# A two-layer gated transformer block: router norm statistics on ScalarE, the last keys and V evicted there, and a V projection two slots later

## The chip, the cores and the metric

The kernel runs on one core of one Trainium2 chip. The core has a matrix engine (TensorE, PE in the profile; its weight loads are the row PEld), a vector engine (VectorE, DVE), an engine for pointwise functions (ScalarE, ACT), a general one (GpSimd, POOL) and a queue that only issues transfers (SyncE, SP). Each works through its own queue of instructions in order and waits for others by semaphores. Matmul results go to PSUM, of which this kernel uses eight banks of 128 x 512 floats. The metric is the device time of one execution, in microseconds (us).

## What is computed

Four batch elements of 512 tokens, 256 features, 16 heads of 16, pass through two layers. Everything is fp32.

```python
x = x + tanh(g_xattn[0]) * L0_xattn(layernorm(x), ctx, ctx, ...)   # softmax attention with a decay bias
x = x + tanh(g_ffn[0])   * L0_ffn(layernorm(x), ...)               # ternary weights, ReLU, 256 -> 1024 -> 256
x = x + tanh(g_xattn[1]) * L1_xattn(layernorm(x), ctx, ctx, ...)   # q, k and v pass through ReLU
x = x + tanh(g_ffn[1])   * L1_ffn(layernorm(x), ...)               # four experts, top 1, gelu, then a norm

# L1_xattn
qp, kp, vp = relu(q @ Wq.T), relu(k @ Wk.T), relu(v @ Wv.T)
A = softmax(NORM * einsum('bqhd,bkhd->bhqk', qh, kh))
# L1_ffn: the normalized x chooses the expert
logits = x @ W_router
expert_idx = argmax(logits, axis=-1)
# the layernorm in front of each part
m, v = mean(x), var(x)
(x - m) / sqrt(v + 1e-5)
```

The part that the change touches is in the second layer: the norm in front of the router (its mean and variance), the projections of keys and values, and where one of the value projections stands.

## The kernel before

**The loop.** Heads are taken in 32 groups, four for each batch element b of each layer, and a group has four units, so 128 units in all. The main loop runs over u from -4 to 127. In each pass `scores` issues two "quads" of score matmuls for TensorE. A quad holds two matmuls `pm` (scores of a unit six ahead, of which only the row maximum is wanted) and two matmuls `psc` (scores of this unit, which become attention weights). Each score matmul is only 32 rows deep[...]. After a quad come its drains: VectorE reduces each pm to a maximum (L508, `tensor_reduce`), and ScalarE turns each psc into exponentials (L523). After the scores `slot(u)` issues the other work of the pass: in every fourth pass `weighted` (the product of weights and V, called po, L551, copied to oT by ScalarE), two passes later `shifted` (pmT, maxima turned and subtracted from q) and `divided` (pn, the quotient o, added to x), and then jobs from chains.

**Chains.** A chain is a list of jobs (function, cost, gap) with the pass in which it may start and the pass by which it must end. `slot` takes jobs whose time has come, the one due first first, as long as their costs fit into 3.1 us; overdue jobs are taken regardless. The order on every engine is thus the order in which the Python code issues instructions: nothing reorders them later. For the second layer, batch b has its first unit at u0 = 64 + 16 b. The chain of its norm (statistics in two halves, rows, transposes) and of the projection of its first keys and queries may start at u0 - 14; the chain `values`, with two halves of V, may start at u0 - 8 and ends by u0 + 2. The router chain `route(b)` starts at four passes (b = 2: two passes) after the last unit of batch b: first half of the statistics, second half, rows, transposes, logits, ranks. The router of the last batch, b = 3, runs behind the loop.

**Statistics.** `layernorm` returns three jobs. The first two read two row tiles each with `bn_stats` and `bn_aggr` on VectorE (L325, L326). The second ends with `deviations`, some eight small operations of GpSimd on 128 x 4 values that make `rstd` and `off` (minus mean times rstd). The third, on ScalarE (L356), writes the normalized rows: four instructions of 128 x 256.

**PSUM banks.** `bank_psum` takes the next of eight banks in turn, so every product waits until the one eight banks earlier has been read out. Two jobs put two results into one bank and have two engines read it: `values` (L433 on ScalarE, L435 on VectorE, one row tile each) and the keys (`key_half`, L463 on ScalarE and L465 on VectorE, one mask each).

**The passes concerned.** V of batch 2 in u=95. The norm of batch 3, and behind it the router of batch 1, in u=98 to 104, together with the first keys and queries of batch 3 (u=102 and 103). V of batch 3 in u=105 and 106, its second keys in u=109. The router of batch 2 from u=114 on, beside the first matmuls of the experts (pg, L996, copied by ScalarE to ha, L1001).

Of the kernel before, what the change touches and what calls it, by code (L numbers as in the profile page):

```python
# [48 lines left out]
def flamingo_kernel(ctx: ExitStack, tc: tile.TileContext, t: dict, out: bass.AP):  # L49
# [260 lines left out]
        ]  # L310


    def layernorm(src, dst, eps, name, eng=None, meanwhile=None):

        mv = sml.tile([P, NT, 2], F32, tag="mv", name=f"mv_{name}")
        var, rstd, fix, off = (
            sml.tile([P, NT], F32, tag=v, name=f"{v}_{name}") for v in ("var", "rstd", "fix", "off")
        )  # L320

        def half_stats(n0):
            for n in range(n0, n0 + NT // 2):
                st = sml.tile([P, 6], F32, tag="st", name=f"st_{name}{n}")
                nc.vector.bn_stats(st, src[:, n, :])  # L325
                nc.vector.bn_aggr(mv[:, n, :], st)  # L326

        def deviations():

            (nc.vector if meanwhile else nc.gpsimd).tensor_scalar(  # L330
                var, mv[:, :, 1], eps, None, ALU.add
            )
            nc.gpsimd.tensor_tensor(rstd, var, power, ALU.pow)
            if meanwhile:
                meanwhile()
            g = nc.vector if meanwhile else nc.gpsimd
            g.tensor_tensor(fix, rstd, rstd, ALU.mult)
            g.tensor_tensor(fix, fix, var, ALU.mult)
            g.tensor_scalar(fix, fix, -0.5, 1.5, ALU.mult, ALU.add)
            g.tensor_tensor(rstd, rstd, fix, ALU.mult)  # L340
            if eng is None:
                nc.gpsimd.tensor_scalar(off, mv[:, :, 0], -1.0, None, ALU.mult)
                nc.gpsimd.tensor_tensor(off, off, rstd, ALU.mult)

        def first():
            half_stats(0)

        def second():
            half_stats(NT // 2)
            deviations()  # L350

        def rows_(dst=dst):
            for n in range(NT):
                r = rstd[:, n : n + 1]
                if eng is None:
                    nc.scalar.activation(  # L356
                        dst[:, n, :], src[:, n, :], AF.Identity, bias=off[:, n : n + 1], scale=r
                    )
                else:
                    eng.tensor_scalar(  # L360
                        dst[:, n, :], src[:, n, :], mv[:, n, 0:1], r, ALU.subtract, ALU.mult
                    )

        return first, second, rows_
# [26 lines left out]
    def prepare(layer, b, eng=None, meanwhile=None):  # L391

        nm = f"a{layer}_{b}"
        st = {}

        def stats():
            st["xn"] = act.tile([P, NT, D], F32, tag="xn", name=f"xn_{nm}")
            first, st["more"], st["rows"] = layernorm(
                x[b], st["xn"], 1e-5, nm, eng, meanwhile
            )  # L400
            first()

        def more_stats():
            st["more"]()

        def norm():
            st["rows"]()

        def turn():
            xTs[layer, b] = act.tile([P, NC, S], F32, tag="xT", name=f"xT_{nm}", bufs=2)  # L410
            transposed(st["xn"], xTs[layer, b], nm, layer == 0 and b > 0)

        def values(n0):
            def run():
                wv = attn_w[layer]["wv"]
                vh = v_sb[b % 2][1]
                pv = bank_psum(f"pv{nm}{n0}")
                for n in range(2):
                    for c in range(NC):
                        nc.tensor.matmul(  # L420
                            pv[:, ts(n, D)], lhsT=cT[b][:, c, ts(n0 + n, P)], rhs=wv[:, c, :],
                            start=(c == 0), stop=(c == NC - 1),
                        )
                if layer == 0:
                    nc.scalar.copy(
                        vh[:, n0 : n0 + 2, :, 0:DK], pv.rearrange("p (n h d) -> p n h d", n=2, d=DK)
                    )
                    return
                for n in range(2):
                    to = vh[:, n0 + n, :, 0:DK]  # L430
                    of = pv[:, ts(n, D)].rearrange("p (h d) -> p h d", d=DK)
                    if n == 0:
                        nc.scalar.activation(to, of, AF.Relu)  # L433
                    else:
                        nc.vector.tensor_scalar(to, of, 0.0, None, ALU.max)  # L435

            return run

        return (
            [(stats, 0, 0), (more_stats, 0, 1), (norm, 0, 1), (turn, 0.9, 1)],  # L440
            [(values(0), 1.75, 0), (values(2), 1.75, 0)],
        )

    def project(layer, b, tt):

        nm = f"{layer}_{b}{tt}"

        def product(w, src, name):
            pp = bank_psum(f"{name}{nm}")
            for c in range(NC):  # L450
                nc.tensor.matmul(  # L451
                    pp, lhsT=attn_w[layer][w][:, c, ts(tt, P)], rhs=src[:, c, :],
                    start=(c == 0), stop=(c == NC - 1),
                )
            return pp

        def key_half(pk, e):
            k = act.tile([P, S], F32, tag="k", name=f"k{nm}{e}", bufs=5)
            h = half[:, e : e + 1]
            if layer == 0:  # L460
                nc.vector.scalar_tensor_tensor(k, pk, h, kext[tt, e], ALU.mult, ALU.add)
            elif e == 0:
                nc.scalar.activation(k, pk, AF.Relu, bias=kone[:, e : e + 1], scale=h)  # L463
            else:
                nc.vector.tensor_scalar(k, pk, h, kone[:, e : e + 1], ALU.mult, ALU.max)  # L465
            ks[layer, b, tt, e] = k

        def keys(between=None, halves=range(2)):
            pk = product("wk", cT[b], "pk")
            if between:  # L470
                between()
            for e in halves:
                key_half(pk, e)

        def queries():
            pq = product("wq", xTs[layer, b], "pq")
            for e in range(2):
                q = act.tile([P, S], F32, tag="q", name=f"q{nm}{e}", bufs=4)
                h = half[:, e : e + 1]
                if layer == 0 and (e == 0 or b < 2):  # L480
                    nc.scalar.activation(q, pq, AF.Identity, bias=bqk[:, 0, tt, e : e + 1], scale=h)  # L481
                elif layer == 0:
                    nc.vector.tensor_scalar(q, pq, h, bqk[:, 0, tt, e : e + 1], ALU.mult, ALU.add)
                elif e == 0:
                    nc.scalar.activation(q, pq, AF.Relu, scale=h)
                else:
                    nc.vector.tensor_scalar(q, pq, h, 0.0, ALU.mult, ALU.max)
                qs[layer, b, tt, e] = q

        return [(keys, 1.75, 1), (queries, 1.75, 0)]  # L490
# [214 lines left out]
    def route(b, eng=None):  # L705
# [3 lines left out]
        def stats():  # L709
            st["xn"] = act.tile([P, NT, D], F32, tag="xn", name=f"xn_f1_{b}")  # L710
            first, st["more"], st["rows"] = layernorm(
                x[b], st["xn"], 1e-5, f"f1_{b}", eng
            )
            first()

# [305 lines left out]
    def chain(steps, start, end, *after):  # L1021
        last = [end] * len(steps)
        for i in range(len(steps) - 2, -1, -1):
            last[i] = last[i + 1] - max(steps[i + 1][2], 1 if steps[i][1] and steps[i + 1][1] else 0)
        c = dict(steps=list(zip(steps, last)), ready=start, after=after, done=None)
        chains.append(c)
        return c
# [12 lines left out]
    for layer in range(2):  # L1040
        for b in range(B):
            u0 = first_unit(layer, b)
            lead, values = prepare(layer, b)
            if (layer, b) == (0, 1):
                *early, early_rows, turn_1 = (job for job, *_ in lead)
                (early_values, *_), later_values = values
                turned_1 = chain([later_values, (turn_1, 0.9, 1)], 1, 4)
                chain(project(layer, b, 0), 5, u0 - LEAD - 2, turned_1)
            elif u0:
                chain(  # L1050
                    [*lead, *project(layer, b, 0)], u0 - 14, u0 - LEAD - 2,
                    ffns[b] if layer else None,
                )
                chain(values, u0 - 8, u0 + 2)
            chain(project(layer, b, 1), max(u0 - 4, 0), u0)
    (totals1, *_), *quant1 = quantize(w1f, "w1")
    (totals2, *_), *quant2 = quantize(w2f, "w2")
# [291 lines left out]
```

## Time and profile before

| what | us |
|---|---|
| median of three runs | 862.4 (861.65 to 863.38) |
| the profiled execution | 861.21 |
| its span, from the first to the last instruction | 859.5 |
| reductions of pm, L508, 512 of 682 ns | 316.9 busy |
| exponentials of psc, L523, 512 of 602 ns | 267.1 busy |
| `bn_stats` of the router norms, L325, 32 of 406 ns | 13.0 busy |
| `bn_aggr` of the same, L326, 32 of 182 ns | 5.8 busy |
| second key halves, L465, 8 of 810 ns | 6.5 busy |
| second V halves, L435, 8 of 424 ns | 3.4 busy |

A line of groups gives source line, engine and operation, what is written from what, the shape and the count; behind the bar stand the busy time in us, the mean ns of one, and the idle time of the engine before it with what ended it. A line of the timeline gives start and duration in us, then the same names. A line of the busy times by stretch gives start and end, length, and for each engine busy time and number of instructions. A line of waits gives who waited for whom, the sum in us, how often, and the longest. Matmul ends are modelled, and a busy PE isn't a PE at its peak.

### The profile page before, as it was taken

How to read it: one execution, taken by the hardware profiler on the slowest of the kernel's cores; microseconds unless marked ns; L12 is line 12 of the kernel's file. 1: busy time of each engine (PE TensorE's matmuls, PEld its weight loads, DVE VectorE, ACT ScalarE, POOL GpSimd, SP SyncE). 2: the span in 40 equal slices, each digit the busy share in tenths (PEclk: the TensorE clock that was granted, in tenths of full speed). 3: DMA queues.
4: the chain of work that ended last, by engine and by line, in shares of the span. 5: the costliest groups of instructions: out<-in, count | busy, mean ns of one | idle time of the engine just before them, and what ended most of it. 6: DMA issues, size and time to landing. Idle time of an engine off the chain costs nothing. (4 is left out here: it accounts for less than half of the span.)

```text
span 859.5 us, 13597 instructions
## 1 busy us (share of the span) xinstructions
PE 821.1 (96%) x5241; PEld 462.1 (54%) x5241; DVE 561.7 (65%) x1218; ACT 422.5 (49%) x886; POOL 277.4 (32%) x446
## 2 busy tenths in 40 slices
PE   6999999999999999999999999999999996999994
PEld 3444454445464346445554445634545655888993
DVE  6878778766857784768646865577877645753443
ACT  2576475553555452655435563357556564223331
POOL 5536365424342422311100120012033216244542
PEclk9999999999999999999999999999999998899998
DMA  8100000000000000000000010001032328136540
GB/s 312 64 1 1 1 2 2 1 1 0 2 13 25 1 1 0 26 0 2 1 1 25 1 50 1 1 1 50 1 119 96 106 75 292 40 93 233 195 155 14
DMA packets 18096, 43.07 MB, mean 50 GB/s; under 512 B 2222, under 2 KB 12208, under 8 KB 15600
## 3 DMA queue, kind: packets, MB, share of 16 engines
q0 software_dynamic: 5488, 28.13, 9.6%
q1 hardware_dynamic: 12128, 13.54, 4.7%
q8 instruction: 41, 0.67, 0.3%
q10 hardware_dynamic: 416, 0.54, 0.2%
q14 instruction: 23, 0.19, 0.1%
HBM read 35.91 MB, written 6.68 MB: 50 GB/s over the span
## 5 line engine op out<-in xcount | busy, mean ns | idle before, releaser
L508 DVE TENSOR_REDUCE m<-pm 128x1 f32<-128x512 f32 x512 | 316.9, 682 | 107.6 <-PE psc L494 105.2
L523 ACT ACTIVATE p<-psc 128x512 f32<-128x512 f32 x512 | 267.1, 602 | 150.9 <-PE psc L494 148.3
L494 PE MATMUL psc<-q,k 32*128 32x512 f32 x1024 | 279.5, 622 | 0.2 <-DVE h L672 0.2
L494 PE MATMUL pm<-k,q 32*128 32x512 f32 x1024 | 262.1, 615 | 1.3 <-ACT q L481 0.9
L526 POOL TENSOR_TENSOR p<-p,dec 128x256 f32<-128x256 f32 x128 | 93.6, 735 | 177.2 <-ACT p L523 177.2
L494 PEld LDWEIGHTS pm<-k,q 32*128 32x128 f32 x1024 | 92.7, 184 | 83.5 <-issue 50.0
L494 PEld LDWEIGHTS psc<-q,k 32*128 32x128 f32 x1024 | 106.6, 183 | 52.2 <-issue 25.7
L551 PE MATMUL po<-p,v 128*32 128x512 f32 x1024 | 116.5, 595 | 1.9 <-DVE m L508 1.9
L551 PEld LDWEIGHTS po<-p,v 128*32 128x32 f32 x1024 | 31.7, 109 | 81.8 <-issue 60.8
L996 PE MATMUL pg<-xs,wg 128*128 128x128 f32 x608 | 72.4, 276 | 1.8 <-ACT xs L977 1.3
L996 PEld LDWEIGHTS pg<-xs,wg 128*128 128x128 f32 x608 | 70.5, 192 | 5.9 <-issue 1.7
L1178 PE MATMUL pyf<-wo,ha 128*128 128x256 f32 x304 | 70.3, 387 | 0.0
L1009 ACT ACTIVATE ha<-pg,wg 128x128 f32<-128x128 f32 x120 | 34.2, 368 | 69.6 <-PE pg L996 66.8
L619 POOL TENSOR_TENSOR x<-x,o 128x256 f32<-128x256 f32 x14 | 10.2, 729 | 174.4 <-DVE o L612 131.7
L1178 PEld LDWEIGHTS pyf<-wo,ha 128*128 128x128 f32 x304 | 57.9, 195 | 7.5
L664 PE MATMUL ph<-xTf,w1q 128*128 128x512 f32 x128 | 60.0, 605 | 0.0
L379 PE MATMUL py_f<-w2q,h 128*128 128x256 f32 x256 | 57.2, 381 | 0.0
L557 ACT COPY oT<-po 128x512 f32<-128x512 f32 x32 | 18.7, 584 | 77.6 <-PE po L551 77.6
L379 PEld LDWEIGHTS py_f<-w2q,h 128*128 128x128 f32 x256 | 48.0, 190 | 9.4 <-DVE m L508 3.0
L451 PE MATMUL pk<-cT,wk 128*128 128x512 f32 x68 | 35.3, 644 | 7.2 <-DMA cT<-in_ctxT_dram 7.2
L1182 DVE TENSOR_TENSOR y<-y,pyf 128x256 f32<-128x256 f32 x19 | 8.0, 421 | 47.4 <-PE pyf L1178 43.4
L664 PEld LDWEIGHTS ph<-xTf,w1q 128*128 128x128 f32 x128 | 22.6, 189 | 30.4 <-issue 18.2
(223 smaller groups left out, 810.1 us busy)
## 6 DMA issues: line engine op xcount, KB each, us to landing
x<-in_x_dram SPq DMA_DIRECT2D x4, 512.0 KB, 7.0
rows_d<-xn_f SPq DMA_DIRECT2D x4, 512.0 KB, 3.0
rows_d<-x SPq DMA_DIRECT2D x4, 512.0 KB, 3.1
cT<-in_ctxT_dram SPq DMA_DIRECT2D x3, 512.0 KB, 9.5
w1q<-in_w_dram SPq DMA_DIRECT2D x1, 1024.0 KB
w2q<-in_w_dram SPq DMA_DIRECT2D x1, 1024.0 KB, 11.3
wo<-in_wo_dram SPq DMA_DIRECT2D x2, 512.0 KB
rows<-in_rows_dram SPq DMA_DIRECT2D x1, 640.0 KB, 9.2
```

The costliest lines, as they stand in the source:

```text
L379: nc.tensor.matmul(py[:, n, :], lhsT=operand(c, n0 + n), rhs=w[:, c, :], start=(c == 0), stop=(c == chunks - 1),)
L451: nc.tensor.matmul(pp, lhsT=attn_w[layer][w][:, c, ts(tt, P)], rhs=src[:, c, :], start=(c == 0), stop=(c == NC - 1),)
L494: nc.tensor.matmul(out_, lhsT=lhs[r, ts(n, P)], rhs=rhs[r, :], start=True, stop=True)
L508: nc.vector.tensor_reduce(m[:, n, 2 * pair + i, r : r + 1], pm[i], AX.X, ALU.max)
L523: nc.scalar.activation(p[:, i, :], psc[i], AF.Exp, scale=SCALE)
L526: nc.gpsimd.tensor_tensor(d, d, dec.unsqueeze(1).to_broadcast([P, 2, P]), ALU.mult)
L551: nc.tensor.matmul(po[i * HP : (i + 1) * HP, :], lhsT=v_sb[b % 2][0][:, kt, c0 : c0 + HP], rhs=ps_exp[NT * s + kt, i // 2][:, i % 2, :], s ...
L557: nc.scalar.copy(pos[s], po)
L664: nc.tensor.matmul(ph, lhsT=w1q[:, c, ts(f, P)], rhs=st["xT"][:, c, :], start=(c == 0), stop=(c == NC - 1),)
L996: nc.tensor.matmul(ph[:, f, :], lhsT=w[:, c, ts(f2 * NF // 2 + f, P)], rhs=xs[j][:, c, :], start=(c == 0), stop=(c == NC - 1),)
L1009: nc.scalar.activation(ha[:, f, :], (ha if src is None else src)[:, f, :], AF.Gelu, bias=biases[j][:, fa : fa + 1],)
L1178: nc.tensor.matmul(py, lhsT=hs[j, f // 4][:, f % 4, :], rhs=wo1[f // 4][:, f % 4, :], start=(f == 0), stop=(f == NF - 1),)
```

## The change

The router norms of batches 1 and 2 get their mean and variance another way. Instead of `bn_stats` and `bn_aggr` on VectorE, ScalarE passes four times over the rows with the function Identity, summing each row as it goes; GpSimd makes minus the mean of the sums; then ScalarE passes four times more with Square and that as its bias, and GpSimd makes the variance plus eps. All eight passes write their (unused) values into one tile `dump`. Each group of four takes the place in the chain that one half of the statistics had. The router norms of batches 0 and 3 and all other norms stay as they were.

The keys and values of the last batch (3) in the second layer are evicted by ScalarE alone.

The chain of V for batch 2 may start at u0 + 1 rather than u0 - 8, and its two halves are two passes apart; in the order as built they move from u=95 to u=97 and u=99.

```diff
+        def total(half):
+            if half == 0:
+                made["tot", name] = sml.tile([P, 2, NT], F32, tag="tot", name=f"tot_{name}", bufs=1)
+                made["dump", name] = wts.tile([P, D], F32, tag="h", name=f"dump_{name}", bufs=8)
+            tot, dump = made["tot", name], made["dump", name]
+            for n in range(NT):
+                if half == 0:
+                    nc.scalar.activation(
+                        dump, src[:, n, :], AF.Identity, accum_out=tot[:, 0, n : n + 1]
+                    )
+                else:
+                    nc.scalar.activation(
+                        dump, src[:, n, :], AF.Square, bias=off[:, n : n + 1],
+                        accum_out=tot[:, 1, n : n + 1],
+                    )
+            if half == 0:
+                nc.gpsimd.tensor_scalar(off, tot[:, 0, :], -1.0 / D, None, ALU.mult)
+            else:
+                nc.gpsimd.tensor_scalar(var, tot[:, 1, :], 1.0 / D, eps, ALU.mult, ALU.add)
...
         def first():
-            half_stats(0)
+            total(0) if sums else half_stats(0)
         def second():
-            half_stats(NT // 2)
+            total(1) if sums else half_stats(NT // 2)
             deviations()
...
-                    if n == 0:
+                    if n == 0 or b == B - 1:
                         nc.scalar.activation(to, of, AF.Relu)
...
-            elif e == 0:
+            elif e == 0 or b == B - 1:
                 nc.scalar.activation(k, pk, AF.Relu, bias=kone[:, e : e + 1], scale=h)
...
             first, st["more"], st["rows"] = layernorm(
-                x[b], st["xn"], 1e-5, f"f1_{b}", eng
+                x[b], st["xn"], 1e-5, f"f1_{b}", eng, sums=0 < b < B - 1
             )
...
-                chain(values, u0 - 8, u0 + 2)
+                late = (layer, b) == (1, B - 2)
+                chain(
+                    [(job, cost, 2 * int(late)) for job, cost, _ in values],
+                    u0 + 1 if late else u0 - 8, u0 + 3 if late else u0 + 2,
+                )
```

In `deviations` the two operations that made `var` and the first form of `off` from the old statistics are left out where `sums` is set.

More of the change, by code (lines that the diff above doesn't have):

```diff
@@ L310, in quantize, with layernorm @@
         ]
-    def layernorm(src, dst, eps, name, eng=None, meanwhile=None):
+    def layernorm(src, dst, eps, name, eng=None, meanwhile=None, sums=False):
         mv = sml.tile([P, NT, 2], F32, tag="mv", name=f"mv_{name}")
@@ L326, in half_stats @@
                 nc.vector.bn_aggr(mv[:, n, :], st)
+        def total(half):
[17 more added lines that the diff above has]
+                nc.gpsimd.tensor_scalar(var, tot[:, 1, :], 1.0 / D, eps, ALU.mult, ALU.add)
         def deviations():
-            (nc.vector if meanwhile else nc.gpsimd).tensor_scalar(
-                var, mv[:, :, 1], eps, None, ALU.add
-            )
+            if not sums:
+                (nc.vector if meanwhile else nc.gpsimd).tensor_scalar(
+                    var, mv[:, :, 1], eps, None, ALU.add
+                )
             nc.gpsimd.tensor_tensor(rstd, var, power, ALU.pow)
@@ L341, in deviations @@
             if eng is None:
-                nc.gpsimd.tensor_scalar(off, mv[:, :, 0], -1.0, None, ALU.mult)
+                if not sums:
+                    nc.gpsimd.tensor_scalar(off, mv[:, :, 0], -1.0, None, ALU.mult)
                 nc.gpsimd.tensor_tensor(off, off, rstd, ALU.mult)
         def first():
-            half_stats(0)
+            total(0) if sums else half_stats(0)
         def second():
-            half_stats(NT // 2)
+            total(1) if sums else half_stats(NT // 2)
             deviations()
@@ L1053, in flamingo_kernel @@
                 )
-                chain(values, u0 - 8, u0 + 2)
+                late = (layer, b) == (1, B - 2)
+                chain(
+                    [(job, cost, 2 * int(late)) for job, cost, _ in values],
+                    u0 + 1 if late else u0 - 8, u0 + 3 if late else u0 + 2,
+                )
             chain(project(layer, b, 1), max(u0 - 4, 0), u0)
```

## The prediction, made before the run

> **What bounds the kernel now.** Times below are in us from the start of the span; "u=97" is the pass of the main loop with that index. I read the page's busy line first, then the busy time in six stretches, the waits of two of them, and the timeline.
>
> The page, busy time by engine:
>
> ```profile
> PE 821.1 (96%) x5241; PEld 462.1 (54%) x5241; DVE 561.7 (65%) x1218; ACT 422.5 (49%) x886; POOL 277.4 (32%) x446
> ```
>
> Busy time in chosen stretches (u=95 and 96; 97 to 100; 101 to 104; 115 and 116):
>
> ```profile
> core 0: us, PE busy (x) PEld busy (x) DVE busy (x) ACT busy (x) POOL busy (x), PEclk, DMA share, GB/s
> 552.10:563.30 11.20, 11.20 (x81) 5.54 (x80) 6.57 (x11) 4.90 (x10) 0.00 (x0) 1.00 0.01 1
> 563.30:579.60 16.30, 15.31 (x111) 6.83 (x107) 14.07 (x32) 9.24 (x17) 3.17 (x9) 1.00 0.00 1
> 579.60:596.60 17.00, 16.84 (x104) 8.45 (x101) 13.56 (x27) 14.00 (x28) 5.54 (x10) 1.00 0.18 63
> ...
> 647.80:657.40 9.60, 9.50 (x81) 4.61 (x80) 7.20 (x17) 5.30 (x10) 3.49 (x9) 1.00 0.01 2
> ```
>
> TensorE is the bound over all, and the 49% of ScalarE hides that in u=101 to 104 it is busy 14.00 of 17.00. In u=97 to 100 it is VectorE, 14.07 of 16.30, and TensorE waits for it, as the waits of that stretch say:
>
> ```profile
> PEld pm L494 <- DVE m L508: 2.9, 5, 1.3
> ...
> PEld po L551 <- DVE m L508: 1.3, 1, 1.3
> ```
>
> ScalarE's own timeline in u=101 to 103 is a chain nearly without a gap; the exponentials stand behind every norm:
>
> ```profile
> 580.20 2.07 ACT L356 ACTIVATE xn_a<-x,off_a,rstd_a 128x256 f32<-128x256 f32 x4
> 582.17 2.03 ACT L523 ACTIVATE p<-psc 128x512 f32<-128x512 f32 x4
> 584.08 0.60 ACT L372 COPY xT_a<-pt_a 128x512 f32<-128x512 f32 x1
> 584.55 1.12 ACT L523 ACTIVATE p<-psc 128x512 f32<-128x512 f32 x2
> ...
> 588.65 0.78 ACT L463 ACTIVATE k<-pk,kone,cols 128x512 f32<-128x512 f32 x1 [1.67 <-PE pk L451]
> 589.32 2.06 ACT L356 ACTIVATE xn_f<-x,off_f,rstd_f 128x256 f32<-128x256 f32 x4
> 591.29 2.03 ACT L523 ACTIVATE p<-psc 128x512 f32<-128x512 f32 x4
> ```
>
> The eight PSUM banks go round in order, so a score matmul waits for the drain of the one eight banks earlier: the pm of u=102 (583.02 on) use the psc banks of u=101, and follow those exponentials (582.77, 583.28 ends).
>
> [...]here PE shows 15.31 of 16.30 busy in the very stretch where it stalls[...]. [...]here the second half of each key waits for the first on ScalarE:
>
> ```profile
> L465 DVE TENSOR_SCALAR k<-pk,cols,kone 128x512 f32<-128x512 f32 x8 | 6.5, 810 | 8.8 <-ACT k L463 8.8
> ```
>
> **The price of a pass.** [...]The accumulating kind is shown at 512 columns:
>
> ```profile
> L276 ACT ACTIVATE abs_w<-w1q x4: 649/657/665, 32.6 to 40.6; 128x512 f32<-128x512 f32 x4
> L276 ACT ACTIVATION_READ_ACCUMULATOR abs_w<-w1q x4: 220/228/237, 33.2 to 41.2; 128x1 f32 x4
> ```
>
> Two of them start 0.61 apart (32.65, 33.26). [...]1.6 for the four of total(0), 1.95 for total(1). That is the low end. But all passes write one dump tile, so the second to fourth wait for the one before on the same engine: [...]at most 0.6 and 0.7, so 2.4 and 2.8. I take 2.1 and 2.5.[...] No table load is counted.
>
> **Part 1, V of batch 2.** It leaves u=95, where it took 554.05 to 557.70 of PE, 3.65, for u=97 and u=99. The quads of u=96 then wait for u=95's reductions (553.24 + 4 x 0.61, last bank free at 555.75), so po begins at 556.9 rather than 559.75: 2.85 gained. In u=97 to 100 VectorE gets two evictions of 0.42. Each starts 2.45 after its pva (556.50 - 554.05), pva some 1.95 after the quads, so at 4.4; the four reductions ahead of it end at 1.15 + 2.44 = 3.6; VectorE stands about 0.75 each time and the next reductions queue behind. 0.84 + 1.5 + 0.15 of small waits = 2.5, in a stretch that VectorE bounds: the po of u=100 comes 0.35 early. Ends: 2.0 gained (only the 0.84 is lost) to 0.5 lost.
>
> **Part 2, batch 1's statistics.** VectorE loses 4 x (0.40 + 0.18) less overlap = 1.08 twice. The first (577.67) lay beside po, 576.01 to 579.58, and is worth nothing; the second (583.74) delays reductions by 0.6, which ScalarE's delay covers. On ScalarE total(0) stands after xn_a and before the exponentials of u=101, total(1) after the xT copy and before those of u=102. Walking the queues: exponentials of u=101 582.17 to 583.9 (+2.1 - 0.35); pm of u=102 583.02 to 584.5; its last psc waits for the xT copy, so pmT 585.79 to 587.4; total(1) ends at 588.85, the exponentials of u=102 at 590.8 (586.97); both key halves now on ScalarE, done 592.2 (590.27); pq 591.38 to 593.3. Rstd takes POOL 2.94 from the statistics (584.99 to 587.93), so xn_f 589.32 to 592.1, exponentials of u=103 591.29 to 594.1, q 593.40 to 596.1, the xTf copy of VectorE ends 598.15 (595.47), and the last psc of u=104, which had waited for just that copy (595.52), starts at 598.2; po 596.57 to 599.2. Parts 1 and 2 together: +2.65; at low and high pass prices +1.7 and +3.3. The 2.36 of x with beta on POOL (591.46) and SP's two stores move by as much, and nobody waits for them.
>
> **Part 3, last keys and V.** The second V eviction in u=106 is gone from VectorE (ended 611.29; a psc follows at 611.34): -0.4. In u=105 a reduction waits for PE anyway, and in u=109 VectorE's q waits for ScalarE's q, which waits for PE: 0. ScalarE has room at all three.
>
> **Part 4, batch 2's statistics.** The timeline at u=115:
>
> ```profile
> 647.60 0.42 DVE L619 TENSOR_TENSOR x<-x,o 128x256 f32<-128x256 f32 x1
> ...
> 647.94 0.58 ACT L1001 COPY ha<-pg 128x512 f32<-128x512 f32 x1 [2.05 <-PE pg L996]
> ...
> 649.14 2.06 ACT L523 ACTIVATE p<-psc 128x512 f32<-128x512 f32 x4 [0.61 <-PE psc L494]
> 649.23 0.59 PE L494 MATMUL psc<-q,k 32*128 32x512 f32 x2
> ```
>
> Total(0) needs x (648.02) and stands before the ha copy, which so ends at 650.65 rather than 648.52. The last psc of u=115 takes that pg bank: it begins 650.7 against about 648.85; pg's second half 649.94 to 651.65 (+1.7). Total(1) again stands before a ha copy, 652.02 to 655.05, whose bank the last psc of u=116 takes: another 1.05; po 653.85 to 656.6, +2.75. Low and high: 1.75 and 3.4. The po behind it lets ScalarE catch up but gives PE nothing back. VectorE's gain is 0.2, as its reductions start at 649.22 and could at 649.0. POOL: off goes ahead of the copy of b (642.72), used only at 703; a row gather (656.38) and wg (662.71, used 683) move by up to 3 and keep their lead.
>
> **Sum.** 2.65 - 0.4 + 2.75 = +5.0 on the profiled execution's own 861.21 (span 859.5), so 866.2; the median of the runs is 862.4, 1.2 above it: 867.4. With the low ends and V at its best 862.4 + 3.05 - 1.6 = 863.8; high ends, V at its worst 869.6. What a measurement here can tell from no change is about 0.2%, 1.7 us.
>
> **Rivals.** B, faster, one mechanism: VectorE alone holds PE in 563 to 597, and the passes fit in ScalarE's gaps. VectorE loses 2.15 of statistics, 0.81 of k and its 0.7 wait there, and gains 0.84: -2.8, with part 3 -3.2: 859.2. For it: 14.07 of 16.30, ScalarE at 49%. Against it: in 579.6 to 596.6 the gaps are 3.0 and the passes need 4.6. It decides if the passes cost PE under about 1.5. C, no change: V keeps 2.85 - 0.84 = 2.0 and the passes are at their low end: 1.7 - 1.65 + 1.75 - 0.4 = +1.4 less the 0.6 of the second statistics: 863.2. For it the uncertain waits of part 1; against it both must come together. D, the change does more than it says: Square not in the loaded table, two loads of 1.28 (the trace's row) per batch on a full ScalarE, +5: 872. The trace shows no Square[...].
>
> **Numbers.** A (as worked out) 0.62, B 0.22, C 0.12, D 0.04. Predicted 867.4; A's own range is 863.8 to 869.6. The range 860.3 to 870 leaves out most of B (0.15) and D. Faster 0.22; same 0.12 (most of C, the edge of A); slower 0.66.
>
> **What would show it.** Right: exponentials of u=101 some 2 later against the end of xn_a, pm of u=102 waiting for ScalarE, the distance from po of u=100 to po of u=104 3 longer, from u=115 to po of u=116 2.7 longer; in u=97 and 99 VectorE's v waiting for ScalarE's. Wrong: pitch of a pass under 0.45, po of u=100 over 1.5 early against u=95, or no wait of PE for ScalarE there.

## The result, and the profile after

The changed kernel takes 868.36 us (median of four runs, 867.38 to 868.83), the kernel before 862.22 beside it: ratio 1.0068, 95% interval 1.0051 to 1.0085. It is slower by some 5.9 us; 867.4 had been predicted. The profiled execution took 868.33 us, its span 866.6.

The page of the changed kernel, busy time by engine:

```profile
PE 824.5 (95%) x5241; PEld 462.5 (53%) x5241; DVE 555.2 (64%) x1198; ACT 432.8 (50%) x922; POOL 278.1 (32%) x446
```

VectorE lost 6.5 us of work and ScalarE gained 10.3: the totals show only that work has moved from a busier engine to a less busy one, and don't show that this costs 6 us. The stretches do. Busy time of the changed kernel in the four stretches that answer to those shown of before (u=95 and 96; 97 to 100; 101 to 104; 115 and 116):

```profile
core 0: us, PE busy (x) PEld busy (x) DVE busy (x) ACT busy (x) POOL busy (x), PEclk, DMA share, GB/s
553.60:561.90 8.30, 8.30 (x66) 2.98 (x65) 5.62 (x9) 4.24 (x8) 0.00 (x0) 1.00 0.01 2
561.90:580.75 18.85, 17.85 (x127) 8.85 (x123) 13.99 (x30) 9.83 (x19) 3.19 (x9) 1.00 0.00 1
580.75:601.25 20.50, 17.86 (x102) 8.82 (x98) 12.03 (x22) 19.14 (x45) 5.54 (x10) 1.00 0.15 51
652.20:664.60 12.40, 11.58 (x81) 4.83 (x80) 5.18 (x9) 9.19 (x26) 3.78 (x10) 1.00 0.00 1
```

The first stretch is 2.9 us shorter than before (11.20), the second 2.55 longer (16.30), the third 3.5 longer (17.00), the last 2.8 longer (9.60). In the third, ScalarE went from 14.00 of 17.00 to 19.14 of 20.50 busy: it is now the bound there, and TensorE waits. ScalarE's timeline in that stretch shows a batch's eight passes, each an ACTIVATE and a read of its accumulator, in two groups ahead of exponentials:

```profile
581.36 2.08 ACT L379 ACTIVATE xn_a<-x,off_a,rstd_a 128x256 f32<-128x256 f32 x4
583.34 0.40 ACT L336 ACTIVATE dump_f<-x 128x256 f32<-128x256 f32 x1
583.64 0.19 ACT L336 ACTIVATION_READ_ACCUMULATOR dump_f<-x 128x1 f32 x1
583.86 0.42 ACT L336 ACTIVATE dump_f<-x 128x256 f32<-128x256 f32 x1
...
585.36 2.04 ACT L546 ACTIVATE p<-psc 128x512 f32<-128x512 f32 x4
...
587.74 0.55 ACT L340 ACTIVATE dump_f<-x,off_f 128x256 f32<-128x256 f32 x1
...
588.40 0.51 ACT L340 ACTIVATE dump_f<-x,off_f 128x256 f32<-128x256 f32 x1
...
590.18 2.04 ACT L546 ACTIVATE p<-psc 128x512 f32<-128x512 f32 x4
592.83 1.45 ACT L486 ACTIVATE k<-pk,kone,cols 128x512 f32<-128x512 f32 x2 [0.61 <-PE pk L474]
```

The sums take 583.34 to 585.36, 2.02 us, the squares 587.74 to 590.18, 2.44. TensorE's timeline shows who waits for the exponentials behind them; both waits are missing from the kernel before:

```profile
585.99 0.70 PE L517 MATMUL pm<-k,q 32*128 32x512 f32 x2 [1.74 <-ACT p L546]
...
590.81 1.98 PE L474 MATMUL pk<-cT,wk 128*128 128x512 f32 x4 [0.73 <-ACT p L546]
```

At batch 2 ScalarE's timeline reads as predicted. The passes wait for x, and the copies ha queue behind them:

```profile
652.51 0.42 ACT L336 ACTIVATE dump_f<-x 128x256 f32<-128x256 f32 x1 [2.23 <-DVE x L642]
...
654.54 0.57 ACT L1024 COPY ha<-pg 128x512 f32<-128x512 f32 x1
655.01 2.06 ACT L546 ACTIVATE p<-psc 128x512 f32<-128x512 f32 x4
...
659.36 0.56 ACT L1024 COPY ha<-pg 128x512 f32<-128x512 f32 x1
```

and the last psc of u=116 in TensorE's timeline waits for the bank of that copy:

```profile
659.98 1.12 PE L517 MATMUL psc<-q,k 32*128 32x512 f32 x2 [0.82 <-ACT ha L1024]
```

One thing has to be kept apart when two such profiles are laid beside each other. In this execution of the changed kernel everything stands 1.5 us later already at the first po (52.32 against 50.77), where the two programs are the same. TensorE's granted clock, a share of full speed and the third number from the end of a line, differs there. From 29 to 32 us of the kernel before, and of the changed kernel:

```profile
29.00:32.00 3.00, 3.00 (x24) 1.35 (x22) 1.36 (x3) 1.86 (x4) 2.32 (x4) 1.00 0.04 8
...
29.00:32.00 3.00, 3.00 (x15) 1.26 (x17) 0.00 (x0) 0.59 (x1) 2.25 (x3) 0.50 0.03 8
```

In the changed kernel's execution the half clock lasts 3.4 us (28.8 to 32.3). The 14 profiles of this study fall into two groups up to u=90, where all the programs are the same: in seven, the changed kernel's among them, the first matmul of pn in u=90 starts at 518.6 to 518.8 us, in the other seven, with the kernel before, at 517.2 to 517.5. So I compare distances. One mark is good for it, the first matmul of pn, every fourth pass. The distances between its starts, in us, read from TensorE's timeline (profiles of the experiments below included):

| kernel | u=90 to 98 | 98 to 102 | 102 to 106 | 106 to 110 | 110 to 114 | 114 to 122 | 122 to 130 |
|---|---|---|---|---|---|---|---|
| before | 51.41 | 17.71 | 20.83 | 21.57 | 16.83 | 37.19 | 23.74 |
| changed | 49.65 | 21.18 | 22.26 | 21.28 | 16.89 | 39.98 | 23.47 |
| no sums | 49.66 | 19.15 | 21.27 | 21.29 | 17.95 | 37.03 | 23.46 |
| late V only (again) | 49.65 | 19.16 | 20.83 | 21.57 | 17.93 | 37.01 | 23.47 |
| sums ahead of oT | 49.65 | 19.15 | 22.26 | 21.28 | 16.06 | 40.06 | 23.46 |
| batch 2 later | 49.64 | 21.19 | 22.26 | 21.28 | 16.06 | 37.91 | 24.30 |
| V on ScalarE, 97 and 99 | 49.59 | 18.47 | 21.27 | 21.29 | 16.05 | 37.27 | 23.47 |
| V on ScalarE, 98 and 99 | 48.49 | 18.32 | 21.27 | 21.28 | 16.05 | 37.27 | 23.47 |
| same, keys as before | 48.51 | 18.32 | 20.79 | 21.29 | 16.88 | 37.18 | 23.47 |

The column for "130" ends at the last pn, just behind the loop. The column 110 to 114 lies beside the expert weights' transfers and swings between 16.05 and 18.6 over all profiles, and by 1.1 us for one and the same program; it is left out of what follows. So are, here, four kernels whose clock was at half for a while from u=101 on; the last section has them.

### The profile page after: what moved, and what is told of

Its sections match the earlier page's. It is cut to its first block, busy times and chain, and to the rows that moved or that the text cites. A ratio compares the mean times of both kernels' runs of the same rounds, so it can differ in the third digit from the quotient of the medians.

```text
span 866.6 us, 13607 instructions
## 1 busy us (share of the span) xinstructions
PE 824.5 (95%) x5241; PEld 462.5 (53%) x5241; DVE 555.2 (64%) x1198; ACT 432.8 (50%) x922; POOL 278.1 (32%) x446
```

## The experiments

The theory of the prediction: an accumulating pass costs what it delays in ScalarE's queue, where exponentials and bank drains stand behind it, and what VectorE is relieved of is worth nothing. Its main rival: VectorE is what holds TensorE there, and the other parts (late V, evictions) matter as much.

### Parts alone: without the statistics, the statistics alone, one batch's

Without the statistics (late V and the evictions of b = 3 stay):

```diff
-                x[b], st["xn"], 1e-5, f"f1_{b}", eng, sums=0 < b < B - 1
+                x[b], st["xn"], 1e-5, f"f1_{b}", eng
```

> The change without its ScalarE statistics (all norms keep bn_stats): late V and the last batch's keys and V on ScalarE stay. Theory (the passes before the exponentials cost, V gives almost nothing): V -0.35, V of batch 3 -0.4, the second key half in front of xn_f up to +0.6, so 862.0, between 861.3 and 862.8; po of u=100 some 0.3 early against u=95's start. Rival (the late V in a stretch bound by VectorE is what costs, the passes are harmless): +4 to +6, 866 to 868. Rival (every us off VectorE counts): -1.7, 860.5.

The statistics alone (V in u=95 and all second halves on VectorE, as before):

```diff
-                    if n == 0 or b == B - 1:
+                    if n == 0:
...
-            elif e == 0 or b == B - 1:
+            elif e == 0:
...
-                late = (layer, b) == (1, B - 2)
+                late = False
```

> The kernel before with the ScalarE statistics of batches 1 and 2 alone. Theory: batch 1 +3.0 to 3.5, batch 2 +2.75, so about +6, 868.2 (867.3 to 869). Rival (late V costs): -1 to +1.5, 861 to 863.7.

And the statistics of batch 1 only:

```diff
-                x[b], st["xn"], 1e-5, f"f1_{b}", eng, sums=0 < b < B - 1
+                x[b], st["xn"], 1e-5, f"f1_{b}", eng, sums=b == 1
```

> The change with ScalarE statistics for batch 1 only; batch 2 keeps bn_stats. Theory: the loss at u=115 and 116 goes, 2.8 less than the change: 865.5 (864.7 to 866.3). Rival (batch 2's passes lie in ScalarE's idle time and cost nothing): like the change, 868.4.

Measured: without the statistics 0.9998 (0.9987 to 1.001), the statistics alone 1.0066 (1.0053 to 1.0079), batch 1's only 1.0036 (1.0022 to 1.0049). So the slowdown is the statistics, all of it. In the table the changed kernel and the one without statistics differ by 2.03 in 98 to 102 (the four sums, 2.02 long: paid in full), by 0.99 in 102 to 106 (the four squares, 2.44 long, which ScalarE's 1.67 us of waiting for pk, seen before, take up in part) and by 2.95 in 114 to 122 (batch 2). That is 6.0 in sum. The times expected above start from 862.2 for the kernel before; it took 863.7 beside these runs, so the differences are what to compare: -0.2 us for no sums (-0.2 expected), +5.7 for the statistics alone (+6.0), +3.1 for batch 1's (+3.3).

### The pass: one dump tile or two

The author had estimated a pass at 0.40 us (neighbours overlap) to 0.6 (each waits for the one before, because all write one tile). Here neighbours write two halves of a tile twice as wide:

```diff
-                made["dump", name] = wts.tile([P, D], F32, tag="h", name=f"dump_{name}", bufs=8)
+                made["dump", name] = wts.tile([P, 2 * D], F32, tag="h", name=f"dump_{name}", bufs=8).rearrange("p (i d) -> p i d", d=D)
...
-                        dump, src[:, n, :], AF.Identity, accum_out=tot[:, 0, n : n + 1]
+                        dump[:, n % 2, :], src[:, n, :], AF.Identity, accum_out=tot[:, 0, n : n + 1]
...
-                        dump, src[:, n, :], AF.Square, bias=off[:, n : n + 1],
+                        dump[:, n % 2, :], src[:, n, :], AF.Square, bias=off[:, n : n + 1],
```

> The change with two halves of the dump tile used in turn, so that a pass need not wait for the one before it. Theory: pitch of a pass from 0.53 to 0.40 and from 0.64 to 0.49, 0.5 and 0.6 off each group of four, up to 1.1 off per batch: 866.2 to 867.4. If the passes wait for each other through something else than the dump tile, the pitch stays and the time is 868.4.

Measured 1.0038 (1.0024 to 1.0052), where the change has 1.0068. ScalarE's timeline with two dump halves:

```profile
582.01 0.41 ACT L336 ACTIVATE dump_f<-x 128x256 f32<-128x256 f32 x1
582.32 0.19 ACT L336 ACTIVATION_READ_ACCUMULATOR dump_f<-x 128x1 f32 x1
582.41 0.40 ACT L336 ACTIVATE dump_f<-x 128x256 f32<-128x256 f32 x1
...
585.99 0.53 ACT L340 ACTIVATE dump_f<-x,off_f 128x256 f32<-128x256 f32 x1
...
586.49 0.51 ACT L340 ACTIVATE dump_f<-x,off_f 128x256 f32<-128x256 f32 x1
```

The next pass starts 0.40 us after the one before (0.53 with one tile), with Square 0.49 to 0.50 (0.64 to 0.66). The four sums now take 1.60 us, the four squares 1.97: the low ends of the prediction (1.6 and 1.95) were the prices without the dependence. The last pass of a group has no pass behind it, so a tile that nobody reads cost 0.13 to 0.15 us at three places in each of four groups, some 1.8 us of ScalarE's queue. The ratio fell by 2.6 us in the mean; the two intervals just touch, so it fits, and the surplus isn't shown to be real. In the profile 114 to 122 falls by 1.1 us (38.86 against 39.98). In 98 to 106 nothing is seen of it (43.57 against 43.44); but TensorE's clock was at half there for 3.4 us of this execution.

### The same passes in another place

In the next kernel nothing is different but the order of one group: batch 1's sums stand ahead of the copy oT<-po, where ScalarE was idle for 3.05 us, waiting for po.

```diff
+            if u in (first_unit(1, 2) + 4,):
+                c = ahead if u == first_unit(1, 2) + 4 else routed
+                c["steps"].pop(0)[0][0]()
+                c["ready"], c["done"] = u + c["steps"][0][0][2], u
             weighted(u // NT - 1)
```

> The changed kernel with nothing moved but one group: batch element 1's four sum passes stand ahead of the copy oT<-po in ScalarE's queue, not behind it, in the 3.05 us in which ScalarE is idle for TensorE's po. The theory that a pass costs what it delays in ScalarE's queue gives back this group's 2.1 us: ratio about 1.0043 where the change has 1.0068. The rival, that the passes cost by what GpSimd and the norm behind them finish later or by a contention that follows them, gives no difference: 1.0068.

Measured 1.0035 (1.0021 to 1.0049). ScalarE's timeline of this kernel:

```profile
577.72 0.44 ACT L336 ACTIVATE dump_f<-x 128x256 f32<-128x256 f32 x1
...
579.69 0.19 ACT L336 ACTIVATION_READ_ACCUMULATOR dump_f<-x 128x1 f32 x1
580.91 0.58 ACT L580 COPY oT<-po 128x512 f32<-128x512 f32 x1 [1.04 <-PE po L574]
581.39 2.08 ACT L379 ACTIVATE xn_a<-x,off_a,rstd_a 128x256 f32<-128x256 f32 x4
583.37 2.03 ACT L546 ACTIVATE p<-psc 128x512 f32<-128x512 f32 x4
```

The passes end at 579.88, and the copy still waits 1.04 us for po. The exponentials start at 583.37 in place of 585.36, in a profile that is level with the changed kernel's to 0.03 us at u=90. In the table 98 to 102 falls from 21.18 to 19.15, to the hundredth what it is without any sums. That tells both things: the place was the cost of the sums, and VectorE's relief from the first half of the statistics is worth nothing, as these are gone here and present in the kernel without sums. The rival of VectorE as the only bound falls with it.

The same was tried for batch 2, with the router norm two passes later so that its sums fall into ScalarE's wait for the po of u=116:

```diff
-            routed = chain(route(b), u0 + 2, u0 + 9)
+            routed = chain(route(b), u0 + 5, u0 + 10)
...
+            if u in (first_unit(1, 3) + 4,):
+                c = ahead if u == first_unit(1, 2) + 4 else routed
+                c["steps"].pop(0)[0][0]()
+                c["ready"], c["done"] = u + c["steps"][0][0][2], u
             weighted(u // NT - 1)
```

> The changed kernel with batch element 2's router norm begun two slots later: its sum passes in ScalarE's idle time behind po of u = 116, its squares in u = 117, and all that follows up to the routing two slots later. If ScalarE's queue is the cause, the sums' 2.0 us come back and the squares cost at most their 2.5 us less the idle time of u = 117: ratio 1.0040 to 1.0045. If the delayed routing is what counts, the dispatch behind it is late and the time stays or grows: 1.0068 or more.

Measured 1.0058 (1.0044 to 1.0072): better than the change by 0.9 us in the mean, with intervals that overlap, and worse than I expected. The table says why: 114 to 122 comes back from 39.98 to 37.91, the 2.1 us expected, but 122 to 130 grows from 23.47 to 24.30. All that follows the routing stands later, and the dispatch's products come a pass later in TensorE's queue. Both theories were half right.

### The late V, and the keys

First nothing but the late V (the kernel before with this one part):

```diff
-                chain(values, u0 - 8, u0 + 2)
+                late = (layer, b) == (1, B - 2)
+                chain(
+                    [(job, cost, 2 * int(late)) for job, cost, _ in values],
+                    u0 + 1 if late else u0 - 8, u0 + 3 if late else u0 + 2,
+                )
```

> The kernel before with nothing but the third V two slots later (u = 97 and 99, second halves on VectorE). The prediction's part 1 says that 2.85 us gained at u = 96 are given back in u = 97 to 100 but for 0.35 us: ratio 0.9996. The rival, that only VectorE's 0.84 us of evictions are given back, says 2.0 us: 0.9977.

> The run with nothing but the late third V, once more. Its profile shows it 0.33 us ahead from u = 102 on, at most 0.6 at u = 126, while its runs gave 1.8 us (0.9979). If the profile's stretch is the whole effect, the ratio now is 0.9993 to 0.9996 and the rest was how the runs fell; if the 1.8 us are the change's, it is 0.998 again, and something behind u = 126 gains that the prediction did not count.

The first time it gave 0.9979 (0.997 to 0.9988), for which the rival's number stood. Its profile said otherwise: from u=90 to u=102 it gained 0.33 us. Run once more, with 21 runs, it gave 0.9994 (0.9987 to 1.0002), and its profile a gain of 0.31. So the small gain stands, and most of the 1.8 us was not the change's. That it came from how the runs fell, as some executions have the early half clock and some don't, is likely but not shown. Of the first gain nearly all is lost again in u=97 to 100. VectorE's timeline of the first of these runs shows the two evictions with the waits that the prediction had put at 0.75:

```profile
566.29 0.43 DVE L458 TENSOR_SCALAR v<-pva 128x256 f32<-128x256 f32 x1 [0.73 <-ACT v L456]
...
575.05 0.42 DVE L458 TENSOR_SCALAR v<-pva 128x256 f32<-128x256 f32 x1 [0.71 <-ACT v L456]
```

If VectorE loses this, V evicted by ScalarE alone should keep it. Two kernels without the statistics, the second with the first half of V one pass later (u=98 and 99; its expectation calls this the second half one slot earlier, but the edit moves the first):

```diff
-                    if n == 0 or b == B - 1:
+                    if n == 0 or b >= B - 2:
```

> The change without ScalarE's statistics, and with both halves of the third V (b = 2) cleared on ScalarE, so that VectorE has no V eviction in u = 97 to 100 and no wait of 0.7 us for ScalarE's half ahead of it. The theory that VectorE's work sets the end of u = 99/100 (0.42 + 0.71 us stand there ahead of a norm's statistics) gives 1.4 us less than the kernel before: ratio about 0.998. The rival, that the wait of the next reductions for TensorE covers it, gives no difference: 1.000. A loss over 0.5 us would mean that ScalarE's own queue is now late.

```diff
-                    [(job, cost, 2 * int(late)) for job, cost, _ in values],
-                    u0 + 1 if late else u0 - 8, u0 + 3 if late else u0 + 2,
+                    [(job, cost, 1 * int(late)) for job, cost, _ in values],
+                    u0 + 2 if late else u0 - 8, u0 + 3 if late else u0 + 2,
```

> As the run before it, with the third V's second half one slot earlier (u = 98 and 99 in place of 97 and 99). If ScalarE has room in both slots, what the V move frees at u = 96 (2.9 us) is kept to a larger part: 2 us less than the kernel before, ratio 0.9975. If the room is filled by TensorE's own products there, it ends as the run before it does.

Measured 0.9986 (0.9978 to 0.9993) and 0.9984 (0.9976 to 0.9991): both are faster than the kernel before, by 1.2 and 1.4 us. The times don't part them from each other; the table does. From 90 to 102 the first takes 68.06 us, the second 66.81, against 68.81 without the statistics and 69.12 before. So to take V from VectorE brought 0.75 us, and the other pass for its first half 1.25 more. Why that pass is better was not tested.

Last the keys. In both, the last keys' second half is on ScalarE, ahead of xn_f. Here it is back on VectorE, once in the second of these kernels and once in the changed kernel:

```diff
-            elif e == 0 or b == B - 1:
+            elif e == 0:
```

> As the run with the third V at u = 98 and 99 on ScalarE, but with the last keys' second halves on VectorE again, as in the kernel before. Theory: the second key half on ScalarE stands ahead of xn_f in u = 102 and delays the exponentials behind it by 0.45 us (591.29 became 591.74 in the run without statistics), so this gives 0.4 us more: ratio about 0.998, from 0.9984. Rival: the 0.81 us and the wait on VectorE that come back cost as much: 0.9984 or a little over.

> The changed kernel with nothing undone but the keys: the last keys' second halves on VectorE as before. If the half microsecond by which batch element 1's stretch lost more than predicted is the second key half on ScalarE ahead of xn_f, this gives it back: 0.4 to 0.5 us, ratio 1.0063. If it is the wait of TensorE's pk for the exponentials behind the passes, it stays: 1.0068.

Measured 0.997 (0.9958 to 0.9982) and 1.0062 (1.0048 to 1.0076). The first is the best kernel of this study, 2.6 us below the kernel before. Its ratio is taken against the same executions of that kernel as the first one of the late V, so it may flatter; but the distances from u=90 to 110 fall by 2.6 as well (108.91 against 111.52). ScalarE's timeline with both key halves there, V at u=98 and 99:

```profile
586.71 1.45 ACT L486 ACTIVATE k<-pk,kone,cols 128x512 f32<-128x512 f32 x2 [1.66 <-PE pk L474]
588.05 2.06 ACT L379 ACTIVATE xn_f<-x,off_f,rstd_f 128x256 f32<-128x256 f32 x4
```

and with one:

```profile
586.53 0.78 ACT L486 ACTIVATE k<-pk,kone,cols 128x512 f32<-128x512 f32 x1 [1.67 <-PE pk L474]
587.21 2.06 ACT L379 ACTIVATE xn_f<-x,off_f,rstd_f 128x256 f32<-128x256 f32 x4
```

From the start of k to that of xn_f it is 1.34 and 0.68 us, and 102 to 106 falls from 21.27 to 20.79. So this half on ScalarE costs 0.48 us. In the changed kernel the gain by the ratios is 0.5 us in the mean, but the interval holds zero as well, and the two theories of that run are not told apart by its time. Its profile shows the same 0.48: from the keys' eviction to the pn of u=106 it takes 18.43 us (594.83 to 613.26, all of it at full clock), against 18.91 (592.83 to 611.74).

## Why the prediction was right

The sum was +5.0 on the profile's own time, and the parts, in distances from u=95 on, came out thus:

| step | predicted | measured |
|---|---|---|
| po of u=96 | -2.85 | -2.90 |
| po of u=100 (part 1) | -0.35 | -0.33 |
| po of u=104 (parts 1 and 2) | +2.65 | +3.19 |
| from there to po of u=108 (part 3) | -0.4 | -0.34 |
| from there to po of u=116 (part 4) | +2.75 | +2.85 |
| four sums, four squares | 2.1, 2.5 | 2.02, 2.44 |

The steps measured add up to 5.7, the ratio of the runs says 5.9, and 5.0 were predicted; most of the difference is Part 2's. The 1.2 us that the prediction put on top are the distance from the profiled execution of the kernel before to its median; that execution is one of those without the early half clock.

**Part 1.** The gain, the two waits of VectorE for ScalarE's half and what they give back were right in place and size, and the run with the late V alone bears out the sum. Without these waits (V on ScalarE) 0.75 us more of the gain is kept, and 2.0 when V's first half is moved on by a pass as well.

**Part 2.** The price of the passes, their place in the queue and TensorE's new wait for the exponentials of u=101 are as predicted. The size is 0.54 us off, and the walk through the queues tells where. Taking off the 1.48 us by which this execution is late, the exponentials of u=102 begin at 588.70 (predicted 588.85), but the keys are done at 592.80 (592.2). Between the two stands the wait of 0.73 us that TensorE's pk has for these exponentials: pk takes a PSUM bank that they have to empty first. I had let pk start without it. All later marks of the walk keep about this half microsecond, to po at 599.76 (predicted 599.2). That this wait is the cause is read from the trace; no kernel was run in which pk alone is free of it, and the run with the keys back on VectorE, whose expectation named it as a rival, shows only that the key half costs another 0.48, which the walk had in it.

**Rivals.** The faster one needed VectorE as the only bound; the kernel without sums and the one with the sums moved show the same 19.15 with and without VectorE's first statistics. VectorE isn't without weight in that stretch, as V taken off it was worth 0.75 us, but the relief that the change brings there was worth nothing. No change needed the late V to keep 2.0 us; it kept 0.33. For Square no table is loaded: the changed kernel has two loads of 1.28 us, as the kernel before has, one at the start (at 1.84 us in both) and one for the gelu behind the loop (at 709.10; before, 702.18).

**Part 4.** ScalarE's queue passed the delay on through the ha copies, not x, as predicted, and the end is right: from the pn of u=114 on, taking off the 4.39 us by which that stands later, the second of these ha copies begins at 654.97 (predicted 655.05) and po at 656.64 (656.6). One link was wrong. The last psc of u=115 doesn't wait for the first of these ha copies: it starts at 654.13, before the copy ends (655.11). What waits for the copy is pg's second half (655.18). It is 0.85 late by this, not the 1.7 predicted, and the other 1.94 come at the psc of u=116, for which 1.05 were predicted. That these errors cancel isn't luck: ScalarE has no gap over 0.04 us from the first sum to the second ha copy, so this queue alone sets when that psc starts. What this part didn't foresee is shown by the later router norm: it can't be freed at no cost, because the dispatch at the end of the loop depends on it.

## What to carry over

An engine at 49% of a span can be nearly full in the 17 us where work is added to it, so the place in its in-order queue prices an instruction, not its share of busy time: the same four passes cost 2.0 us ahead of exponentials and nothing in the wait for po. When results are thrown away, give neighbouring instructions different tiles to throw them into (here a pass started 0.40 us after the one before, with one tile 0.53). Look at the granted clock of two profiles before you compare their times (1.5 us here, ahead of any change). And where a ratio and a profile disagree by a microsecond or two, run it again before explaining it.

## What the runs showed of the hardware

**TensorE's clock.** In four of the six profiles with the sums ahead of the exponentials of u=101 (the statistics alone, batch 1's only, two dump halves, the keys back on VectorE), TensorE's granted clock falls just after its wait there. Busy time in stretches of the changed kernel with the keys back on VectorE:

```profile
584.00:586.00 2.00, 0.26 (x3) 0.02 (x2) 0.99 (x2) 1.94 (x8) 0.22 (x1) 1.00 0.01 4
586.00:588.00 2.00, 2.00 (x12) 1.32 (x14) 0.84 (x2) 2.00 (x5) 0.00 (x0) 0.82 0.00 0
588.00:590.00 2.00, 2.00 (x9) 0.50 (x5) 0.91 (x2) 1.90 (x7) 0.00 (x0) 0.50 0.00 0
...
592.00:594.00 2.00, 2.00 (x3) 0.71 (x3) 0.86 (x3) 0.22 (x1) 1.48 (x5) 0.50 0.00 0
```

The column before the last two is the clock. After 2 us with TensorE 0.26 busy it is at half speed for 6.8 us (587.3 to 594.1), and 98 to 102 takes 22.55 where the changed kernel's profile has 21.18 with the clock at 1.00. The ends of the half clock are worked out from the mean clock of such stretches of 2 us: in the four it begins 1.3 to 1.8 us after the wait (of 1.31 us with two dump halves, of 1.74 in the other three) and lasts 3.4 us twice (the statistics alone, two dump halves) and 6.8 twice (batch 1's only, the keys back on VectorE). The same wait of 1.74 us stands in the changed kernel and in the one with batch 2 later, and there the clock stays at 1.00 from 576 to 598. None of the eight profiles without that wait has the dip there.

A wait of 1.94 us stands ahead of the early half clock, and it reads alike in two executions that part behind it: in the kernel before it ends at 27.52 and the clock stays at 1.00, in the changed kernel it ends at 27.53 and the clock is at half from 28.8 on. What decides whether half clock follows a wait was not shown. Where it followed, a stretch could take longer than by the stall alone: here 1.4 us more up to the pn of u=102 (22.55 against 21.18).

**The price of an independent ACTIVATE.** The prediction's low end, 0.40 us from the start of a pass to that of the next, was an estimate of the author's. The trace of the kernel before gives one too. There a COPY from PSUM takes 388 ns with 256 columns (L977) and 584 with 512 (L557), so 256 columns fewer are 0.20 us less, and the accumulating pair of 512 columns starts 0.61 us apart: 0.41, an estimate from these three. At 512 columns ScalarE's instructions from PSUM take 588 ns without a tile for bias or scale (ha, L1001), 687 with one (q, L485) and 779 with two (k, L463). So the bias of Square adds some 0.1, by the same kind of estimate. An Identity pass takes 0.40 to 0.44 us in the traces, its read of the accumulator 0.19. With two dump halves a pass starts 0.40 after the one before, with Square 0.49 to 0.50: the low end was right. The pair in the trace from which it started had this read in it.

**Beside the gathers.** From u=110 to 114, while the expert weights are fetched (DMA share 0.8 to 1.1 in slices of 1 us, for some 7 us), the same work took 16.05 to 18.00 us in 13 profiles (18.61 in one in which the clock dipped as well). In the slices of the kernels without sums and before the clock is 1.00, and some slices of 1 us hold 5 or 6 matmuls, others 10 to 13, though PE shows as busy throughout. The late V alone had 16.83 once and 17.93 the other time, with one and the same program. What holds TensorE there was not settled.
